# Layer 1 attention of a four-layer gated model: scores made once with queries in partitions, weights turned by TensorE

## The chip, the cores and the metric

The kernel runs on one core of a Trainium2 chip. The metric is the device time of one execution in microseconds. The engines are TensorE (PE, with its weight loads as PEld), VectorE (DVE), ScalarE (ACT), GpSimd (POOL) and SyncE (SP), which issues most DMAs. Profiles come from one profiled execution.

## What is computed

Eight batches of 256 query rows by 128 features (`x`) run through four layers. Each adds a gated cross attention over 512 context rows of its batch, and then a gated feed-forward part:

```python
x = x + tanh(g_xattn[0]) * L0_xattn(layernorm(x), ctx, ctx, ...)
x = x + tanh(g_ffn[0])   * L0_ffn(layernorm(x), ...)      # experts, top 2 of 8
x = x + tanh(g_xattn[1]) * L1_xattn(layernorm(x), ctx, ctx, ...)
x = x + tanh(g_ffn[1])   * L1_ffn(layernorm(x), rhs)      # int8 product
...                                                       # layers 2 and 3
```

The change is in `L1_xattn`: 16 heads of 64 features. With query, key and value projections with biases, it is softmax(QK^T / 8) V over the 512 keys for each head and query, and then the output projection with its bias. Everything is f32.

## The kernel before

**Stages.** Layer 0's attention and its experts come first, to about 320 us. During them and into the next stage, the keys and values of layer 1 are projected for all batches and stored in DRAM (`fill`, `k1`, `v1`). After that `pipeline` runs layers 1, 2 and 3 as one loop of steps.

**Units, steps and half steps.** A unit is a layer, a batch `b` and a half `g` of the heads. In layer 1 a unit has eight heads, as four pairs `j`. A unit takes four steps, and a step has two half steps. So a batch of layer 1 is two units, eight steps, 16 half steps, and a pair of heads takes one step. Three streams run side by side: `prepare` (query projections, key and value loads) first, `largest` (the scores' maxima) four steps later, and `attend` (weights and values) eight steps later. One step issues:

```python
next(streams["at"]); self.run_due()      # half step 1: attend; work that is due
next(streams["la"]); self.run_soon()     # maxima; sums and reciprocals
self.some(self.front); self.some(self.back)
next(streams["at"]); next(streams["pr"]) # half step 2: attend; one projection
next(streams["la"]); self.fill2(1)
self.some(self.front); self.some(self.back)
```

`front` is the work ahead of the next batch (`ahead`: gather layer 0's expert rows, add them to `x`, layer normalisation, turn the rows by TensorE in `rows_turned`). `back` is the feed-forward part of a batch that is done (`int8`: normalise, largest per row, round, turn by TensorE, product, add). Both are generators that are advanced one piece in each half step. All instructions of TensorE, VectorE, ScalarE and GpSimd in the pipeline are kept in program order on their engine, and each engine works in order.

**Layer 1 before.** `largest` makes the scores with queries in partitions (`sc<-kx,qx`: 64-row matmuls for the two heads of a pair, 512 keys), and VectorE takes the negated maximum over the keys (`nm<-sc`). Every two pairs, `largest_rows` turns these maxima by TensorE (`pj<-c_f,nm`), splits them into a rounded high part and a rest (`ms`) and writes them by four small DMAs as rows of a tile `m4`. `attend` makes the scores a second time with keys in partitions: a matmul with the constant `up` puts the (negated) maxima of each query into the PSUM tile (`sc<-m,up`), and the scores are added to it (`sc<-qx,kx`). One exponential on ScalarE with a scale of 1/8 gives the weights `et` (`et<-sc`, 128x1024), keys in partitions, as the value matmuls need them. GpSimd adds the weights up (`k<-et`, `total<-k`). A step later `values_of_pair` multiplies by the values (`av<-et,va`), multiplies the totals by ones to sum over partitions (`av<-total,ones`), and VectorE takes the reciprocal and scales (`rec<-av`, `aT`). When both halves of a batch are done, `output1` projects (`pj<-wb,aT`), adds to `x` and hands the batch to `int8`.

**Buffers.** PSUM holds three `sc` tiles of 128x1024, one `pj` and one `av`. `pj` serves query projections (`pj<-xT,wb`, evacuated by ScalarE as `qx<-pj`), transposes of rows, of `nm` and of the int8 rows, the int8 product, and the output projection. A tile is used again when its last reader is done.

Of the kernel before, what the change touches and what calls it, by code (L numbers as in the profile page):

```python
# [31 lines left out]
def bcast(ap, shape):  # L32
    return ap.to_broadcast(list(shape))
# [15 lines left out]
class Flamingo:  # L49
# [60 lines left out]
    def load(self):  # L110
        nc, a = self.nc, self.a
        self.x = self.const("x", [P, NT, D])
        self.ctxT = self.const("ctxT", [D, NB * SK])
        xs = a["x"].rearrange("(t p) d -> p t d", p=P)

        def rows(b):
            nc.sync.dma_start(self.x[:, 2 * b : 2 * b + 2, :], xs[:, 2 * b : 2 * b + 2, :])

        def context(b, eng=nc.sync):
            eng.dma_start(self.ctxT[:, b * SK : (b + 1) * SK], a["ctxT"][:, b * SK : (b + 1) * SK])  # L120


        rows(0)
        context(0, nc.scalar)
        self.w0 = self.loaded("w0", eng=nc.scalar, pool=self.wf0)
        self.b0 = self.loaded("b0", [1, 512], src=a["b0"].unsqueeze(0), eng=nc.scalar, pool=self.wf0)
        self.c_f32 = self.loaded("c_f32")
        self.ident = self.c_f32[:, 0:128]
        self.tri = self.c_f32[:, 128:256]
        self.iota = self.c_f32[:, 256:385]  # L130
        self.up2 = self.c_f32[:, 385:513]
        self.row = self.c_f32[:, 513:514]
        self.g = self.loaded("g", [P, 8], src=a["g"].partition_broadcast(P))
        rows(1)

        self.w1 = self.weights_tile().rearrange("p (k n) -> p k n", k=4)
        self.w1_b = self.loaded("w1_b", eng=nc.scalar)
        nc.sync.dma_start(self.w1[:, 1, :], a["w1"][:, 1, :])
        nc.sync.dma_start(self.w1[:, 2, :], a["w1"][:, 2, :])
        for b in range(2, 4):  # L140
            rows(b)
        for b in range(1, 4):
            context(b)
        for b in range(4, NB):
# [771 lines left out]
    def pipeline(self):  # L916
        nc, tc = self.nc, self.tc
        with ExitStack() as st:
# [3 lines left out]
            self.p_av = st.enter_context(tc.tile_pool(name="p_av", bufs=1, space=PS))  # L922
            self.po = st.enter_context(tc.tile_pool(name="pipe", bufs=2))
            units = [(layer, b, g) for layer in (1, 2, 3) for b in range(NB) for g in range(2)]
            self.due, self.soon, self.back, self.front, self.step, self.kept = [], [], [], [], 0, {}
            streams = {
                n: self.chain(f, units, wait)
# [45 lines left out]
    def run_soon(self):  # L973

        now, self.soon = self.soon, []
        for f in now:
            f()

    def later(self, steps, f):
        self.due.append((self.step + steps, f))  # L980

# [4 lines left out]

    def setup(self, pool):
        nc, a, one = self.nc, self.a, self.one
        self.up = self.t(one, "up", [P, P], F32R)
        nc.vector.tensor_copy(self.up, self.up2)  # L990
        tri8 = self.t(pool, "tri8", [P, 2, SK], U8)
        nc.sync.dma_start(tri8, a["keep_qk"].rearrange("(c p) k -> p c k", p=P))
        self.triq = self.t(one, "triq", [P, 2, SK], BF16)
# [23 lines left out]
        pt = self.pj16()  # L1017
# [106 lines left out]
    def prepare1(self, n, b, g):  # L1124
        nc = self.nc
        xT = self.kept["xT", 1, b]
        qT = self.t(self.po, "qx", [P, 4, S], bufs=3)
        kT = self.t(self.po, "kx", [P, 4, SK], bufs=3)
        self.kept[n] = [qT, kT, None]
        for j in range(4):  # L1130
            f = 4 * g + j
            if j == 0:
                nc.sync.dma_start(kT, self.k1[n])
            if j == 1:
                va = self.kept[n][2] = self.t(self.po, "va", [P, 4, 512], bufs=3)
                nc.sync.dma_start(va, self.v1[n])
            pq = self.pj()
            self.mm2(pq[:, 0:S], self.w1[:, 0, f * P : (f + 1) * P], xT)
            nc.scalar.activation(
                qT[:, j, :], pq[:, 0:S], AF.Identity, bias=self.w1_b[:, 0, f : f + 1]  # L1140
            )
            yield

    def largest(self, n, layer, b, g):
        if layer > 1:
            yield from self.largest23(n, layer, b, g)
            return
        nc = self.nc
        qT, kT, _ = self.kept[n]

        mr = self.t(self.po, "m4", [P, 4, S], bufs=3)
        nc.gpsimd.memset(mr, 0.0)
        self.kept[n][3:] = [mr]
        nm = self.t(self.po, "nm", [P, 2, 2, 2, 2])
        for j in range(4):
            for c in range(2):
                ps = self.sc()
                for z in range(2):
                    h = slice(64 * z, 64 * z + 64)
                    self.mm(ps[:, z, :], qT[h, j, c * P : (c + 1) * P], kT[h, j, :])  # L1160
                nc.vector.tensor_reduce(nm[:, c, j // 2, :, j % 2], ps, AX.X, ALU.max, negate=True)
                if c and j % 2:
                    self.later(1, self.largest_rows(
                        nm, j // 2, 1.0, lambda z, k: mr[64 * z + k : 64 * z + k + 1]
                    ))
                yield

    def largest_rows(self, m, half, scale, row):
# [20 lines left out]
    def attend(self, n, layer, b, g):  # L1189
        if layer > 1:  # L1190
            yield from self.attend23(n, layer, b, g)
            return
        nc = self.nc
        qT, kT, va, mr = self.kept[n]
        mr = mr.bitcast(F32R)
        aT = self.t(self.po, "aT", [P, 4, S], bufs=3)
        self.kept["aT", g] = aT
        for j in range(4):
            ets = []
            half = self.t(self.po, "k4", [P, 2, 2, S])  # L1200
            for k2 in range(2):
                ps = self.sc()
                for z in range(2):
                    h = slice(64 * z, 64 * z + 64)
                    self.mm(
                        ps[:, z, :], self.up[h, :],
                        bcast(mr[h, j, :].unsqueeze(1), [64, 2, S]), True, False,
                    )
                for c in range(2):
                    for z in range(2):  # L1210
                        h = slice(64 * z, 64 * z + 64)
                        self.mm(
                            ps[:, z, c * S : (c + 1) * S],
                            kT[h, j, (2 * k2 + c) * P : (2 * k2 + c + 1) * P], qT[h, j, :],
                            False, c == 1,
                        )
                ets.append(self.weights(ps, 0.125))
                nc.gpsimd.tensor_tensor(half[:, k2], ets[k2][:, :, 0, :], ets[k2][:, :, 1, :], ALU.add)
                if k2:
                    self.later(1, self.values_of_pair(b, 4 * g + j, ets, half, va, aT))  # L1220
                yield

    def weights(self, ps, scale):
        et = self.t(self.po, "et", [P, 2, 2, S], bufs=6)
# [2 lines left out]
        )  # L1227
        return et

    def values_of_pair(self, b, f, ets, half, va, aT):  # L1230
        nc = self.nc
        both = [self.kept["aT", 0], aT]
        total = self.t(self.po, "total", [P, 2, S])
        nc.gpsimd.tensor_tensor(total, half[:, 0], half[:, 1], ALU.add)

        def run():
            po = self.av()
            for c in range(4):
                for z in range(2):
                    at = 64 * (2 * (f % 4) + z)  # L1240
                    self.mm(
                        po[64 * z : 64 * z + 64, 0:S], va[:, c, at : at + 64],
                        ets[c // 2][:, z, c % 2, :], c == 0, c == 3,
                    )
            self.soon.append(lambda: scaled(po))

        def scaled(po):
# [215 lines left out]
    def attend23(self, n, layer, b, g):  # L1463
# [9 lines left out]
        held = {}  # L1473
        for j in range(4):
            for k2 in range(2):
                ps = self.sc()
                for z in range(2):
                    self.mm(
# [249 lines left out]
def arrays_of(i):  # L1728
# [9 lines left out]
            np.eye(P, dtype=f),  # L1738
            (p[:, None] <= p[None, :]).astype(f),
            np.tile(np.arange(P + 1, dtype=f), (P, 1)),  # L1740
            np.tile((p[:, None] % 64 < 2).astype(f), (1, P)),
            p[:, None].astype(f),
        ],
        axis=1,
# [90 lines left out]
```

## Time and profile before

| | us |
|---|---|
| median of 3 runs (range) | 1806.87 (1792.55 to 1807.64) |
| profiled execution | 1792.19 |
| its span, first to last instruction | 1790.4 |
| PE busy in the span | 1558.7 (87%) |
| DVE busy | 1163.2 (65%) |
| ACT busy | 750.8 (42%) |
| POOL busy | 742.8 (41%) |
| mean granted TensorE clock | 0.934 |

In the profile's rows `out<-in` names the tile that is written and those that are read; `L863` and `L867` are the helpers that issue every matmul and every transpose, and `L46` is the one through which the instructions of the other engines go. So groups are told apart by their tiles. An f32 matmul shows as two matmuls. Matmuls overlap, so the pace of TensorE is read from start to start and not from the durations. The first attention of layer 1 begins at about 373 us, and layer 1's last output projection is at 960.7 us.

### The profile page before, as it was taken

How to read it: one execution, taken by the hardware profiler on the slowest of the kernel's cores; microseconds unless marked ns; L12 is line 12 of the kernel's file. 1: busy time of each engine (PE TensorE's matmuls, PEld its weight loads, DVE VectorE, ACT ScalarE, POOL GpSimd, SP SyncE). 2: the span in 40 equal slices, each digit the busy share in tenths (PEclk: the TensorE clock that was granted, in tenths of full speed). 3: DMA queues.
4: the chain of work that ended last, by engine and by line, in shares of the span. 5: the costliest groups of instructions: out<-in, count | busy, mean ns of one | idle time of the engine just before them, and what ended most of it. 6: DMA issues, size and time to landing. Idle time of an engine off the chain costs nothing.

```text
span 1790.4 us, 32118 instructions
## 1 busy us (share of the span) xinstructions
PE 1558.7 (87%) x11760; PEld 773.9 (43%) x11856; DVE 1163.2 (65%) x2667; ACT 750.8 (42%) x1244; POOL 742.8 (41%) x1140
## 2 busy tenths in 40 slices
PE   6886578789999999999998888889889999899995
PEld 2332226234545445445454444445444444444442
DVE  6997542145677676586776686475565665677774
ACT  3553233333233233232333455555545555455543
POOL 4896221234566566465554123232332322422211
PEclk9887688899999999999999899999989999899997
DMA  5443232723121122121222332222121211222210
GB/s 191 157 170 114 86 127 77 227 106 107 53 97 54 49 78 78 48 54 49 72 51 94 72 78 65 49 71 62 39 54 32 58 32 36 53 58 62 67 27 25
DMA packets 65409, 137.77 MB, mean 77 GB/s; under 512 B 12370, under 2 KB 28003, under 8 KB 58596
## 3 DMA queue, kind: packets, MB, share of 16 engines
q1 hardware_dynamic: 63282, 132.03, 23.8%
q0 software_dynamic: 1536, 3.15, 1.3%
q8 instruction: 94, 1.54, 0.4%
q10 hardware_dynamic: 434, 0.54, 0.1%
q14 instruction: 63, 0.52, 0.1%
HBM read 83.50 MB, written 51.38 MB: 75 GB/s over the span
## 4 chain that ended last, share of the span: by engine, by line
PE 58%; DVE 20%; POOL 7%; issue 7%; ACT 5%; DMA 2%; SPq 0%; ACTq 0%; DVEq 0%; POOLq 0%
PE sc L863 31%; PE av L863 13%; PE pj L863 8%; DVE junk L46 5%; PE pj L867 3%; DVE rec L46 2%; PE fl L863 2%; DVE ps L46 2%; DVE pj L46 2%; DVE x L46 2%; DVE nm L46 1%; ACT et L46 1%; POOL lnz L46 1%; DMA kx<-k 1%; POOL k L46 1%
## 5 line engine op out<-in xcount | busy, mean ns | idle before, releaser
L46 ACT ACTIVATE et<-sc 128x1024 f32<-128x1024 f32 (+1 forms) x403 | 405.1, 1005 | 465.0 <-PE sc L863 418.0
L46 DVE CUSTOM_DVE_ANT_0 junk<-sc,m 128x512 bf16<-128x512 f32 x512 | 351.0, 686 | 43.8 <-PE sc L863 30.2
L863 PE MATMUL sc<-qx,kx 64*128 64x256 f32 (+2 forms) x2048 | 269.1, 361 | 13.4 <-DMA qx<-ms 3.1
L863 PE MATMUL sc<-kx,qx 64*128 64x512 f32 (+2 forms) x1024 | 268.9, 561 | 0.7 <-ACT et L46 0.7
L863 PE MATMUL av<-et,va 128*32 128x256 f32 (+1 forms) x3072 | 265.7, 408 | 0.8 <-DVE aT L46 0.8
L863 PEld LDWEIGHTS sc<-qx,kx 64*128 64x128 f32 (+2 forms) x2048 | 179.6, 191 | 139.3 <-issue 120.8
L46 POOL TENSOR_TENSOR k<-et 128x512 f32<-128x512 f32 x128 | 162.6, 1272 | 176.8 <-ACT et L46 174.1
L46 DVE TENSOR_REDUCE nm<-sc 128x2 f32<-128x1024 f32 x128 | 156.1, 1219 | 110.2 <-PE sc L863 110.2
L863 PEld LDWEIGHTS av<-et,va 128*32 128x32 f32 (+1 forms) x3072 | 133.8, 125 | 101.1 <-issue 35.4
L46 POOL TENSOR_TENSOR x<-row,x 128x256 f32<-128x256 f32 x76 | 55.5, 730 | 274.1 <-ACT row L46 260.7
L863 PE MATMUL sc<-m,identb 128*128 128x512 bf16 x416 | 139.7, 400 | 22.0 <-DVE mx L46 12.2
L46 DVE SCALAR_TENSOR_TENSOR ms<-pj,ms 4x256 fp32r<-4x256 f32 x96 | 39.6, 412 | 169.4 <-ACT ms L46 163.1
L863 PEld LDWEIGHTS sc<-kx,qx 64*128 64x128 f32 (+2 forms) x1024 | 87.4, 185 | 87.6 <-issue 66.0
L46 POOL TENSOR_TENSOR lnz<-lny 128x2 f32<-128x2 f32 (+1 forms) x129 | 25.2, 195 | 211.8 <-DVE lny L46 198.4
L46 DVE RECIPROCAL rec<-av 128x256 f32<-128x256 f32 x64 | 111.9, 1748 | 0.0
L46 DVE SCALAR_TENSOR_TENSOR x<-sc,comb,x 128x128 f32<-128x128 f32 x128 | 39.0, 346 | 100.4 <-ACT row L46 100.4
L46 ACT ACTIVATE total<-sc,f_b 128x512 f32<-128x512 f32 x64 | 44.0, 688 | 107.7 <-PE sc L863 107.7
L863 PE MATMUL sc<-xT,wb 128*64 128x512 f32 x256 | 68.9, 614 | 19.0 <-DVE x L46 17.1
L46 POOL TENSOR_TENSOR total<-k 128x512 f32<-128x512 f32 x64 | 81.5, 1273 | 5.0
L863 PEld LDWEIGHTS sc<-wb,total 128*64 128x64 f32 x1024 | 61.6, 137 | 33.6 <-issue 32.6
L863 PE MATMUL sc<-m,up 64*128 64x512 f32 x256 | 75.4, 584 | 0.0
L46 POOL TENSOR_TENSOR aT<-aT,rec 128x512 f32<-128x512 f32 x16 | 20.4, 1273 | 131.8 <-DVE rec L46 131.8
(275 smaller groups left out, 2280.1 us busy)
## 6 DMA issues: line engine op xcount, KB each, us to landing
kx<-k SPq DMA_DIRECT2D x16, 1024.0 KB
va<-v SPq DMA_DIRECT2D x16, 1024.0 KB
k<-fill SPq DMA_DIRECT2D x46, 256.0 KB
v<-fill SPq DMA_DIRECT2D x45, 256.0 KB
pd<-k SPq DMA_DIRECT2D x16, 512.0 KB
kx<-pd SPq DMA_DIRECT2D x64, 128.0 KB
kx<-pd SPq DMA_DIRECT2D x128, 64.0 KB
qx<-pd SPq DMA_DIRECT2D x128, 64.0 KB
```

The source lines that it names most:

```text
L46: return lambda *args, **kw: self.tc.keep_in_program_order(v(*args, **kw))
L863: self.nc.tensor.matmul(out, lhsT, rhs, start=start, stop=stop)
L867: self.tc.keep_in_program_order(self.nc.tensor.transpose(out, in_, ident))
```

## The change

Layer 1's `largest` stream issues nothing; it only keeps its place in the order. `attend` makes the scores once per half step, with queries in partitions: one half `c` of the 256 queries, two heads, 512 keys. VectorE takes the negated maximum, and ScalarE makes the weights with it as a bias, one exponential for each head, into a tile of the `m4` buffers. The division by 8 moves into the query projection (`scale=0.125`, with a scaled bias `bq1`). Two half steps later `turned` transposes these weights by TensorE, eight blocks of 128x128, into an `sc` tile. ScalarE copies that to `et`, and GpSimd adds up in two instructions. In layer 2's `attend23` a call `turn(1)` works off what is left. The values are made for 128 queries at a time. The constant `up2`, the tile `up`, the memset of the rows and layer 1's call of `largest_rows` are gone.

```diff
+    def turn(self, n):
+        if len(self.turns) >= n:
+            self.turns.pop(0)()
...
+        if n == 0:
+            self.bq1 = self.t(self.one, "bq1", [P, 8])
+            nc.gpsimd.tensor_scalar(self.bq1, self.w1_b[:, 0, :], 0.125, None, ALU.mult)
...
             nc.scalar.activation(
-                qT[:, j, :], pq[:, 0:S], AF.Identity, bias=self.w1_b[:, 0, f : f + 1]
+                qT[:, j, :], pq[:, 0:S], AF.Identity, bias=self.bq1[:, f : f + 1], scale=0.125
             )
...
     def largest(self, n, layer, b, g):
...
+            for _ in range(8):
                 yield
...
     def attend(self, n, layer, b, g):
...
+            held = {}
+            for c in range(2):
+                self.turn(2)
                 ps = self.sc()
                 for z in range(2):
                     h = slice(64 * z, 64 * z + 64)
-                    self.mm(
-                        ps[:, z, :], self.up[h, :],
-                        bcast(mr[h, j, :].unsqueeze(1), [64, 2, S]), True, False,
-                    )
-                for c in range(2):
-                    for z in range(2):
-                        h = slice(64 * z, 64 * z + 64)
-                        self.mm(
-                            ps[:, z, c * S : (c + 1) * S],
-                            kT[h, j, (2 * k2 + c) * P : (2 * k2 + c + 1) * P], qT[h, j, :],
-                            False, c == 1,
-                        )
-                ets.append(self.weights(ps, 0.125))
-                nc.gpsimd.tensor_tensor(half[:, k2], ets[k2][:, :, 0, :], ets[k2][:, :, 1, :], ALU.add)
-                if k2:
-                    self.later(1, self.values_of_pair(b, 4 * g + j, ets, half, va, aT))
+                    self.mm(ps[:, z, :], qT[h, j, c * P : (c + 1) * P], kT[h, j, :])
+                nm = self.t(self.po, "nm", [P, 2])
+                nc.vector.tensor_reduce(nm, ps, AX.X, ALU.max, negate=True)
+                p = self.t(self.po, "m4", [P, 4, S], bufs=3).rearrange("p (z k) s -> p z (k s)", z=2)
+                for z in range(2):
+                    nc.scalar.activation(p[:, z, :], ps[:, z, :], AF.Exp, bias=nm[:, z : z + 1])
+                self.turns.append(self.turned(c, p, held, (b, 4 * g + j, va, both)))
                 yield
+
+    def turned(self, c, p, held, of_pair):
+        nc = self.nc
+        def run():
+            ps = self.sc()
+            pt = ps.rearrange("p a (k z s) -> p (a k) z s", k=2, z=2)
+            for k in range(4):
+                for z in range(2):
+                    self.tp(pt[:, k, z, :], p[:, z, k * P : (k + 1) * P], self.ident)
+            et = self.t(self.po, "et", [P, 2, 2, S], bufs=6)
+            nc.scalar.copy(et.rearrange("p a k s -> p (a k s)"), ps.rearrange("p a n -> p (a n)"))
+            held[c] = et.rearrange("p a k (z s) -> p (a k) z s", z=2)
+            if c == 0:
+                held["half"] = self.t(self.po, "k4", [P, 2, 2, S])
+                held["total"] = self.t(self.po, "total", [P, 2, S])
+            half = held["half"][:, c]
+            nc.gpsimd.tensor_tensor(half, et[:, 0], et[:, 1], ALU.add)
+            half = half.rearrange("p k (z s) -> p k z s", z=2)
+            nc.gpsimd.tensor_tensor(
+                held["total"][:, :, c * P : (c + 1) * P], half[:, 0], half[:, 1], ALU.add
+            )
+            if c:
+                self.later(1, self.values_of_pair(held, *of_pair))
+        return run
...
     def values_of_pair(...):
...
-            for c in range(4):
-                for z in range(2):
-                    at = 64 * (2 * (f % 4) + z)
-                    self.mm(
-                        po[64 * z : 64 * z + 64, 0:S], va[:, c, at : at + 64],
-                        ets[c // 2][:, z, c % 2, :], c == 0, c == 3,
-                    )
+            for c in range(2):
+                for k in range(4):
+                    for z in range(2):
+                        at = 64 * (2 * (f % 4) + z)
+                        self.mm(
+                            po[64 * z : 64 * z + 64, c * P : (c + 1) * P], va[:, k, at : at + 64],
+                            held[c][:, k, z, :], k == 0, k == 3,
+                        )
...
     def attend23(...):                      # layers 2 and 3
+                self.turn(1)
                 ps = self.sc()
```

More of the change, by code (lines that the diff above doesn't have):

```diff
@@ L130, in load @@
         self.iota = self.c_f32[:, 256:385]
-        self.up2 = self.c_f32[:, 385:513]
-        self.row = self.c_f32[:, 513:514]
+        self.row = self.c_f32[:, 385:386]
         self.g = self.loaded("g", [P, 8], src=a["g"].partition_broadcast(P))
@@ L924, in pipeline @@
             units = [(layer, b, g) for layer in (1, 2, 3) for b in range(NB) for g in range(2)]
+            self.turns = []
             self.due, self.soon, self.back, self.front, self.step, self.kept = [], [], [], [], 0, {}
@@ L988, in setup @@
         nc, a, one = self.nc, self.a, self.one
-        self.up = self.t(one, "up", [P, P], F32R)
-        nc.vector.tensor_copy(self.up, self.up2)
         tri8 = self.t(pool, "tri8", [P, 2, SK], U8)
@@ L1146, in largest @@
             yield from self.largest23(n, layer, b, g)
[L1147 to L1155, printed above, removed]
-            for c in range(2):
-                ps = self.sc()
-                for z in range(2):
-                    h = slice(64 * z, 64 * z + 64)
[L1160 to L1165, printed above, removed]
+        else:
+            for _ in range(8):
                 yield
@@ L1193, in attend @@
         nc = self.nc
-        qT, kT, va, mr = self.kept[n]
-        mr = mr.bitcast(F32R)
+        qT, kT, va = self.kept[n]
         aT = self.t(self.po, "aT", [P, 4, S], bufs=3)
         self.kept["aT", g] = aT
+        both = [self.kept["aT", 0], aT]
         for j in range(4):
-            ets = []
-            half = self.t(self.po, "k4", [P, 2, 2, S])
-            for k2 in range(2):
+            held = {}
+            for c in range(2):
+                self.turn(2)
                 ps = self.sc()
@@ L1204, in attend @@
                     h = slice(64 * z, 64 * z + 64)
-                    self.mm(
-                        ps[:, z, :], self.up[h, :],
-                        bcast(mr[h, j, :].unsqueeze(1), [64, 2, S]), True, False,
-                    )
-                for c in range(2):
-                    for z in range(2):
-                        h = slice(64 * z, 64 * z + 64)
-                        self.mm(
-                            ps[:, z, c * S : (c + 1) * S],
-                            kT[h, j, (2 * k2 + c) * P : (2 * k2 + c + 1) * P], qT[h, j, :],
-                            False, c == 1,
-                        )
@@ L1228, in weights, with values_of_pair @@
         return et
-    def values_of_pair(self, b, f, ets, half, va, aT):
+    def values_of_pair(self, held, b, f, va, both):
         nc = self.nc
-        both = [self.kept["aT", 0], aT]
-        total = self.t(self.po, "total", [P, 2, S])
-        nc.gpsimd.tensor_tensor(total, half[:, 0], half[:, 1], ALU.add)
+        total, aT = held["total"], both[-1]
         def run():
             po = self.av()
-            for c in range(4):
-                for z in range(2):
-                    at = 64 * (2 * (f % 4) + z)
-                    self.mm(
-                        po[64 * z : 64 * z + 64, 0:S], va[:, c, at : at + 64],
-                        ets[c // 2][:, z, c % 2, :], c == 0, c == 3,
-                    )
+            for c in range(2):
[6 more added lines that the diff above has]
+                        )
             self.soon.append(lambda: scaled(po))
@@ L1740, in arrays_of @@
             np.tile(np.arange(P + 1, dtype=f), (P, 1)),
-            np.tile((p[:, None] % 64 < 2).astype(f), (1, P)),
             p[:, None].astype(f),
```

## The prediction

> **What bounds the kernel now.** The page's first rows come first: TensorE is busy 87% of the span, VectorE 65%, ScalarE 42%, GpSimd 41%. An average over stages says little, so next the stretches. Layer 1's outputs (`pj<-wb,aT`, 64 matmuls) stand at 537.4, 608.7 and 680.0 us in the chain that ended last, one batch (8 steps, 16 half steps) per 71.3 us. The busy times of two such stretches, columns PE, PEld, DVE, ACT, POOL, granted clock, DMA share, GB/s:
>
> ```profile
> 546.25:617.59 71.34, 67.02 (x496) 35.22 (x496) 50.91 (x67) 21.54 (x31) 43.23 (x58) 1.00 0.21 64
> 688.92:760.26 71.34, 67.02 (x475) 35.24 (x476) 48.48 (x65) 21.07 (x30) 43.22 (x58) 0.95 0.21 64
> ```
>
> TensorE is busy 67.0 of 71.3 us, so it sets the pace; ScalarE, 21.5, is nearly free. Its waits there are 2.0 us on `xn`, 1.5 us on `row`, 0.8 us on `ql`. One plain step follows in the timeline; starts are what counts, since durations overlap:
>
> ```profile
> 554.04 1.13 PE L863 MATMUL sc<-kx,qx 64*128 64x512 f32 x4
> 554.61 0.80 PE L863 MATMUL sc<-m,up 64*128 64x512 f32 x2
> 555.24 1.02 PE L863 MATMUL sc<-qx,kx 64*128 64x256 f32 x8
> 556.20 1.95 PE L863 MATMUL av<-et,va 128*64 128x256 f32 x16
> 558.07 1.13 PE L863 MATMUL sc<-kx,qx 64*128 64x512 f32 x4
> 559.13 0.65 PE L863 MATMUL av<-total,ones 128*64 128x256 f32 x4
> 559.72 0.50 PE L863 MATMUL sc<-m,up 64*128 64x512 f32 x2
> 560.05 1.02 PE L863 MATMUL sc<-qx,kx 64*128 64x256 f32 x8
> 561.01 0.65 PE L863 MATMUL pj<-xT,wb 128*64 128x256 f32 x4
> ```
>
> From one query projection (553.46) to the next (561.01) is 7.55 us. Start to start: scores for the largest 1.06, rows of the largest plus second scores 1.29, values 1.87, sums 0.59, projection 0.58.
>
> **The change, part by part.**
>
> *TensorE.* Per half step the `up` matmuls and the second scores go (1.29 us, or 1.1 behind a first score). Eight f32 transposes of 128x128 come. Nearest rows:
>
> ```profile
> 884.69 0.44 PE L867 MATMUL pj<-c_f,xn 128*128 128x128 f32 x2
> 892.91 0.62 PE L867 MATMUL pj<-identb,m 128*128 128x128 bf16 x8
> ```
>
> A lone f32 transpose takes 0.33 us, a pair 0.44, so one more costs 0.11; eight bf16 ones take 0.62, so a run of eight is pipelined. Eight f32: 0.87 plus about 0.16 for the change of shape (between groups above), 1.03 us. The Trainium skill, "TensorE: Matmul & The Clock Gate", Part 4, gives about 275 ns for a transpose in a kernel's context and says that transposes do not count as activity for the full clock. By that rule eight cost 2.2 us, 1.2 us more in each of 128 half steps, +150 us if nothing hides it; by the row, nothing. I take the row: it has eight in one run. The rule stays as the upper end.
> Values become 32 matmuls of 128 columns instead of 16 of 256. The output projection has that shape: 64 in 3.64 us, so 32 take 1.82. No change. A step is then 2x1.03 + 2x1.06 + 1.87 + 0.59 + 0.58 = 7.22 us: **2.6 us less per batch**. Four pairs of transposes of the largest go too, 0.31 us each: **1.25 us less**.
>
> *ScalarE.* One exponential of 1024 (1.02) becomes two of 512 with a bias, by `total<-sc,f_b` 0.69 each, and a copy of 1024, by `m<-pj` 1.01: 2.4 us per half step, 4.8 per step, plus 0.47 for the query copy. It fits in 7.2 as a sum; its order does not (below). *VectorE* keeps its 128 maxima (1.22 us) and loses the 0.41 us halves. *GpSimd*: two of (1.27 + 0.73) per step against three of 1.27; 0.2 us more, beside other work. 128 small DMAs of rows, the memsets (0.95 us) and 64 KB of constants go; they were off the path, I count 0.
>
> *The new wait.* Before, the maxima fed rows that were needed four steps later. Now one half step runs in one chain: scores, maximum (VectorE), two exponentials, all before the next instruction on ScalarE. There, in program order, the query copy `qx<-pj` stands **behind both exponentials**; before, it stood behind one that waited for TensorE alone. It frees `pj`, of which there is one buffer. Whoever uses `pj` right after the projection holds up TensorE, in order, with all behind it. In each batch three do, all in second half steps: the int8 transposes (`pj<-identb,ql`), the int8 product (`pj<-qr,qlT`), and the transposes of the next batch's rows (`pj<-c_f,xn`).
>
> Count from the end of the sums (`av<-total,ones`). TensorE reaches the `pj` user after 1.03 + 1.06 + 0.58 = 2.67 us. ScalarE frees `pj` after reciprocal 1.75, `aT` 0.42, VectorE's side work F that stands before the maximum, maximum 1.22, exponentials 1.38, query copy 0.47, four hand-overs of 0.07: 5.5 + F. The stop is 2.85 + F:
> - int8 product: F = first guess of the root, 0.65. Stop **3.5 us**.
> - rows: F = two `xn`, 1.4 to 2.5. Stop **4.8 us**.
> - int8 transposes: F = two adds of gathered rows (`x<-xT,w,x`, 1.2 each) and two roundings, 2.9. Stop 5.7, and 2 more because the half step before has the other two adds ahead of its own maximum: **7.7 us**.
>
> Together 16.0 us per batch. The present waits of 4.3 us are at the same places or go with the transposes of the largest. Batch: 71.3 - 2.6 - 1.25 - 4.3 + 16.0 = **79.2 us, +7.9**. Elsewhere slack covers the chain: `sc` rotates over three, and a score waits for the copy of the transposes one half step back; from the end of a score to that copy's end is 0.07+1.22+0.07+1.38+0.07+1.01 = 3.8 us, against 6.2 us of TensorE work between (1.87 + 0.59 + 2x1.03 + 1.06 + 0.58).
>
> *The clock.* In layer 3 there is a stop like these:
>
> ```profile
> 1556.26 0.48 PE L867 MATMUL pj<-c_f,xn 128*128 128x128 f32 x1 [3.66 <-POOL xn L46]
> 1558.30 0.80 PE L863 MATMUL sc<-qx,kx 34*128 34x256 f32 x4
> 1567.19 0.50 PE L863 MATMUL sc<-qx,kx 34*128 34x256 f32 x4
> ```
>
> After 3.66 us idle the four score matmuls take 0.80 instead of 0.50, until about 1565. The same page ("Why this matters for your kernels") asks for no gaps over about 3 us; here already 1.54 us before 987.64 (on `ql`) was followed by some 6.5 us of doubled durations. By the page one or two of the three stops lower the clock, by the trace all. A slow period of 6.8 us loses 3.4 us of TensorE work; part falls into waits that exist anyway. I take 2.3 per stop, 7 per batch (0 to 12). Batch: **86.2, +14.9**.
>
> *Ends.* Steps 4 to 7 held eight scores for the largest before any attention; a step took 5.55 us there (350.26 to 355.80), against 3.1 in the steps before. Four such: -10. Filling the first batch without stops: -3. Where layer 2's maxima begin while layer 1 attends, VectorE gets eight maxima of 1.22 on top, with transposes left over for layer 2's first step: +8. Six full batches: 6 x 14.9 = 89.
> Sum: 89 - 10 - 3 + 8 = **+84 us**. The profiled execution took 1792.2 us (span 1790.4): **1876 us**. The median of the runs shown, 1806.9, lies 0.8% above it, the lowest run (1792.6) at it; so this is 3.8% over the median, and runs may scatter some 15 us up.
>
> **The rivals.**
> 1. *Stops, but the clock holds.* For it: 546 to 689 us stays at 1.00 despite waits of 1.5 us. Against: the stop of 3.66. 6 x 7.9 - 5 = +42: 1834 us. 0.20.
> 2. *Transposes are slow or do not count as activity.* Against: eight in 0.62. For: no row shows 16 f32 ones in each step; with the stops, TensorE's counted work would be near half the time and the low clock the rule. +25 per batch, -5: 1937 us. 0.15.
> 3. *The sum of TensorE decides, faster.* `pj` is freed in time because VectorE runs ahead. Then 8 x 3.85 + 10 goes: 1751 us. Against: reciprocal and `aT` alone put the maximum 2.2 us after the sums. This turns slower once the stops exceed 3.85 + 4.3 us a batch. 0.07.
> 4. *Stops half as long* (1.5 to 4 us), the clock mostly held: +0 to +20, 1800 us. 0.10.
> 5. That it does not do what it says: the changed kernel's own instruction order shows the copies, exponentials and `qx` as counted here. Not counted.
>
> **How the numbers follow.** The forecast has 0.48. Its own range: stops 12 to 20 us, clock 3 to 12 per batch, 1840 to 1915. The 8-in-10 range takes in rival 1 and most of 2 and 4: 1812 to 1938. About 1% (18 us) can be told from no change. Faster by over 1%: 0.07; within: 0.09 (most of rival 4); slower: 0.84.
>
> **What would show it.** Layer 1's outputs some 80 to 90 us apart instead of 71.3. Waits of TensorE at `pj<-identb,ql`, `pj<-qr,qlT`, `pj<-c_f,xn` on ScalarE's `qx`, 12 us or more per batch. Transposes of `p` in groups of eight of about 1.1 us. Granted clock in layer 1 clearly under 1.00, ScalarE busy near 45 us a batch. The forecast is wrong if those waits stay under 5 us a batch, or if a group of eight takes over 1.6 us at full clock. Layers 2 and 3 should keep their time.

## The result, and the profile after

The changed kernel takes **1865.7 us** (median of 4 runs, 1861.7 to 1866.0) against 1804.4 us of the kernel before (1792.6 to 1807.6), measured beside it: a ratio of **1.035**, interval 1.030 to 1.040. Predicted were 1876 us and "slower" with 0.84. The profiled executions are 1861.7 us after and 1792.2 us before. The experiments below ran in three sets, each beside the kernel before, whose medians there were 1800.3 to 1802.5 us.

The first three rows of the page after, busy time and share of the span:

```profile
span 1859.8 us, 33621 instructions
## 1 busy us (share of the span) xinstructions
PE 1565.8 (84%) x12560; PEld 838.3 (45%) x12560; DVE 1140.0 (61%) x2634; ACT 888.6 (48%) x1468; POOL 738.6 (40%) x1189
```

TensorE's share fell, although the span grew: it waits more. Two batches of layer 1, from one output (`pj<-wb,aT`) to the next; columns are start and end, length, busy PE, PEld, DVE, ACT, POOL, granted clock, DMA share, GB/s:

```profile
562.45:644.37 81.92, 68.69 (x584) 44.56 (x584) 48.08 (x63) 39.15 (x59) 42.84 (x64) 0.87 0.16 56
644.37:726.29 81.92, 68.70 (x584) 44.56 (x584) 48.07 (x63) 39.14 (x59) 42.82 (x64) 0.87 0.17 56
```

A batch takes 81.9 us instead of 71.3. Idle time rose from 4.3 to 13.2 us, and the granted clock fell to 0.87, so that the busy 68.7 us hold less work than they seem to. What TensorE waited for, 480 to 900 us (total, times, longest):

```profile
PE pj L866 <- ACT qx L46: 43.8, 10, 4.5
PE pj L862 <- ACT qx L46: 16.0, 11, 2.7
PE sc L866 <- ACT m L46: 2.9, 5, 0.6
PE av L862 <- POOL total L46: 2.8, 5, 0.6
```

60 of 66 us stand at `pj`, released by ScalarE's query copy `qx`. The same batch in TensorE's timeline (start, duration, what, and in brackets the idle time before it):

```profile
568.27 1.09 PE L866 MATMUL sc<-c_f,m 128*128 128x128 f32 x8
569.29 1.13 PE L862 MATMUL sc<-kx,qx 64*128 64x512 f32 x4
570.35 0.65 PE L862 MATMUL pj<-xT,wb 128*64 128x256 f32 x4
570.93 1.09 PE L866 MATMUL sc<-c_f,m 128*128 128x128 f32 x8
571.96 1.13 PE L862 MATMUL sc<-kx,qx 64*128 64x512 f32 x4
573.01 1.97 PE L862 MATMUL av<-et,va 128*64 128x128 f32 x32
574.81 0.60 PE L862 MATMUL av<-total,ones 128*64 128x256 f32 x4
575.35 1.09 PE L866 MATMUL sc<-c_f,m 128*128 128x128 f32 x8
...
598.16 0.37 PE L866 MATMUL pj<-identb,ql 128*128 128x128 bf16 x2 [4.23 <-ACT qx L46]
598.32 1.91 PE L866 MATMUL sc<-c_f,m 128*128 128x128 f32 x8
600.16 2.08 PE L862 MATMUL sc<-kx,qx 64*128 64x512 f32 x4
...
610.29 0.37 PE L862 MATMUL pj<-qr,qlT 128*128 128x128 bf16 x2 [2.73 <-ACT qx L46]
...
624.98 0.69 PE L866 MATMUL pj<-c_f,xn 128*128 128x128 f32 x2 [4.54 <-ACT qx L46]
```

The first seven rows are one plain step, from 568.27 to the start of the eighth at 575.35: 7.08 us; it was 7.55. A group of eight transposes occupies 1.02 us, start to start. Then come the three stops of the prediction, 11.5 us together, each followed by rows of twice the duration (1.91 for 1.09, 2.08 for 1.13).

### The profile page after: what moved, and what is told of

It reads as the page before. It is cut to its first block, busy times and chain, and to the rows that moved or that the text cites. A ratio compares the mean times of both kernels' runs of the same rounds, so it can differ in the third digit from the quotient of the medians.

```text
span 1859.8 us, 33621 instructions
## 1 busy us (share of the span) xinstructions
PE 1565.8 (84%) x12560; PEld 838.3 (45%) x12560; DVE 1140.0 (61%) x2634; ACT 888.6 (48%) x1468; POOL 738.6 (40%) x1189
## 3 DMA queue, kind: packets, MB, share of 16 engines
q8 instruction: 100, 1.64, 0.4%
## 4 chain that ended last, share of the span: by engine, by line
PE 44%; DVE 17%; ACT 6%; POOL 4%; issue 4%; DMA 1%; SPq 1%; ACTq 0%; DVEq 0%; POOLq 0%
PE sc L862 20%; PE av L862 12%; PE pj L862 5%; DVE junk L46 4%; DVE rec L46 3%; PE sc L866 3%; DVE nm L46 3%; PE pj L866 2%; ACT m L46 2%; POOL lnz L46 1%; DVE x L46 1%; DVE xn L46 1%; ACT total L46 1%; ACT et L46 1%; POOL k L46 1%
## 5 line engine op out<-in xcount | busy, mean ns | idle before, releaser
L46 ACT ACTIVATE et<-sc 128x1024 f32<-128x1024 f32 (+1 forms) x275 | 273.8, 996 | 147.1 <-PE sc L862 140.8
L862 PE MATMUL av<-et,va 128*64 128x128 f32 (+1 forms) x4096 | 278.6, 356 | 0.0
L46 ACT ACTIVATE m<-sc,nm 128x512 f32<-128x512 f32 x256 | 162.2, 687 | 205.2 <-DVE nm L46 196.1
L862 PEld LDWEIGHTS av<-et,va 128*64 128x64 f32 (+1 forms) x4096 | 188.6, 134 | 109.3 <-issue 67.5
L46 ACT COPY et<-sc 128x1024 f32<-128x1024 f32 x128 | 130.2, 1017 | 103.2 <-PE sc L866 96.1
L866 PE MATMUL sc<-c_f,m 128*128 128x128 f32 x1024 | 155.7, 301 | 3.6 <-ACT m L46 2.9
L866 PEld LDWEIGHTS sc<-c_f,m 128*128 128x128 f32 x1024 | 125.1, 154 | 50.1 <-issue 38.4
L862 PE MATMUL sc<-qx,kx 38*128 38x256 f32 (+1 forms) x1024 | 133.5, 339 | 0.4 <-DMA qx<-ms 0.4
L862 PEld LDWEIGHTS sc<-qx,kx 38*128 38x128 f32 (+1 forms) x1024 | 79.4, 191 | 114.3 <-issue 110.7
L46 POOL TENSOR_TENSOR total<-k 128x256 f32<-128x256 f32 x128 | 93.1, 727 | 10.0
```

The lines of the kernel that those rows point to most:

```text
L46: return lambda *args, **kw: self.tc.keep_in_program_order(v(*args, **kw))
L862: self.nc.tensor.matmul(out, lhsT, rhs, start=start, stop=stop)
L866: self.tc.keep_in_program_order(self.nc.tensor.transpose(out, in_, ident))
```

## The experiments

Theory: the stops come from the query copy queued behind the second half step's exponentials, which wait for VectorE; the stops then bring the half-rate periods. Rivals: TensorE's clock costs nothing beside the waits; the transposes lower the clock; ScalarE's added work binds by itself.

### 1. The projection ahead of the second half step

```diff
-                next(streams["at"])
-                next(streams["pr"])
+                if self.step < 4 * 2 * NB:
+                    next(streams["pr"])
+                    next(streams["at"])
+                else:
+                    next(streams["at"])
+                    next(streams["pr"])
```

> The changed kernel with one edit: while layer 1 lasts, a step's query projection is issued ahead of its second half step of attention instead of behind it. On ScalarE the query copy `qx<-pj` then stands behind the exponentials of the first half step only, and `pj` is free well before the second half step's users come. My theory (the stops come from the query copy queued behind the second half step's exponentials, and the stops bring the half-rate periods): the three stops of 4.2, 2.7 and 4.5 us per batch go under 1 us each, the three half-rate periods per batch go, a batch falls from 81.9 to 63 to 66 us (81.9 - 11.5 - 7.5 = 62.9), the run to about 1735 to 1765 us, under the kernel before. Rival A (transposes and ScalarE's extra work bind, whatever the order): the wait only moves, to `sc` or to the transposed weights, a batch stays over 78 us and the run at 1840 us or more. Rival B (the first half step's exponentials, themselves behind VectorE's side work, hold the query copy as well): stops half as long, 70 to 75 us per batch, about 1800 us.

Measured: **1761.4 us** (1759.9 to 1763.3), ratio to before 0.978 (0.972 to 0.983). Two batches of it, columns as above, then its waits from 480 to 860 us:

```profile
538.40:601.85 63.45, 59.93 (x584) 40.32 (x582) 46.50 (x62) 39.06 (x60) 42.75 (x65) 1.00 0.22 72
601.85:666.93 65.08, 61.57 (x585) 41.20 (x583) 46.50 (x62) 39.06 (x60) 42.72 (x65) 0.97 0.21 70
```

```profile
PE pj L866 <- POOL ql L46: 8.9, 5, 1.8
PE av L862 <- POOL total L46: 4.6, 5, 0.9
PE pj L866 <- DVE xn L46: 4.0, 10, 0.4
```

No wait on `qx` is left, the clock is back, and a batch takes 63.4 us, 18.5 less: 9.7 from waits (13.2 to 3.5), 7.6 from the clock (run 4), and 8 steps of 0.15 us (6.93 from 544.12 to 551.05 against 7.08). ScalarE has the same work, 39.1 us a batch, and there are as many transposes. Rival A falls, and rival B too.

### 2. The exponentials without VectorE's maximum

```diff
-                nc.vector.tensor_reduce(nm, ps, AX.X, ALU.max, negate=True)
...
-                    nc.scalar.activation(p[:, z, :], ps[:, z, :], AF.Exp, bias=nm[:, z : z + 1])
+                    nc.scalar.activation(p[:, z, :], ps[:, z, :], AF.Exp)
+                nc.vector.tensor_reduce(nm, p, AX.X, ALU.max, negate=True)
```

> The changed kernel without the link from VectorE to ScalarE: the exponentials take no bias, and VectorE's maximum (same count and size) is taken from the exponentials' output instead, where nobody waits for it. What is left out: the subtraction of the largest. The order on every engine and all loads stay. My theory (a stop is maximum plus VectorE's side work plus two exponentials plus the query copy): each stop shrinks to about 1.4 us, what two exponentials (1.38) and the copy (0.47) leave beyond the projection; 3 x 1.4 = 4.2 us of stops per batch, the clock loss 0 to 7.5 us: a batch 67 to 75 us, the run 1770 to 1820 us. Rival (ScalarE's own added work of 2.4 us per half step makes the stops, VectorE has no part): stops stay over 3 us each, over 79 us per batch, 1850 us.

Measured: 1761.3 us (1759.0 to 1763.8). One batch:

```profile
596.54:664.51 67.97, 62.82 (x585) 40.34 (x583) 48.03 (x62) 37.21 (x59) 42.77 (x64) 0.97 0.21 67
```

68.0 us, inside 67 to 75: the order on ScalarE alone leaves stops of 1.0 us at most on `qx`, and the link to VectorE makes the rest of them. The run as a whole came out 9 us under the range that I expected, because the first batch (83.7 us for 104.3, from layer 1's ninth projection, where attention begins, to its first output) and the passage to layer 2 (73.3 for 78.9) got shorter as well. The rival (ScalarE's work alone) falls.

### 3. Extra matmuls in the stops, too many

```diff
+    def busy(self, n):
+        ps = self.sc()
+        for k in range(n):
+            self.mm(ps[:, k % 2, :], self.ident[0:64, :], self.ctxT[0:64, 0:512])
...
+        self.busy(7)
         pt = self.pj16()
...
+        self.busy(4)
         po = self.pj()
...
+        if b:
+            self.busy(8)
         self.rows_turned(layer, b, xn)
```

> The changed kernel with 7, 4 and 8 extra f32 matmuls of 64x512 (about 0.53 us each, their result unused) issued just ahead of the int8 transposes, the int8 product and the next rows' transposes, so that TensorE works through most of each stop instead of idling. The waits for `pj` stay as they are. My theory (idle time at the stops brings the half-rate periods, which cost 7.5 us per batch beside the 11.5 us of waiting): granted clock in layer 1 back to 0.95 or more, a batch about 75 us, the run 40 to 50 us shorter, 1815 to 1825 us. Rival 1 (the waiting alone is the loss, the clock costs nothing because VectorE and ScalarE are late anyway): 81.9 us per batch as now, 1862 us or a little more. Rival 2 (transposes don't count as activity and the low clock comes from them): half-rate periods stay, 1860 us or more.

Measured: 1872.4 us (1868.7 to 1879.3), which looks like rival 1. The timeline says otherwise: seven of the extra matmuls took 6.2 us, 0.89 each, not 0.53. My 0.53 came from pairs of scores that use rows 0 to 63 and 64 to 127 in turn; these used the same 64 rows each time. So 16.9 us of extra work stood where the stops were 11.5, 5.4 too much; yet a batch took 79.5 us, 2.4 less. In the profiled total this was lost again: 10 us up to the first output of layer 1 (490.8 us for 480.8), and 16 us behind its last output, where eleven of the extra matmuls stand at places that had no such stop. Inconclusive as a total, so it was sized anew.

### 4. Extra matmuls that fit

```diff
-        self.busy(7)
+        self.busy(4)
...
-        self.busy(4)
+        self.busy(2)
...
-            self.busy(8)
+            self.busy(5)
```

> The run with extra matmuls ahead of the three users of `pj`, sized anew: there one took 0.89 us instead of the 0.53 I had counted, so they filled 16.9 us where the stops were 11.5. Now 4, 2 and 5 of them, 9.8 us, a little under the stops of 4.2, 2.7 and 4.5 us. My theory (the stops bring the half-rate periods): what remains idle at each stop is under 1 us, granted clock 1.00, a batch 74 to 75 us (81.9 less the 7.5 lost to the clock), the run 1810 to 1830 us. Rival 1 (the clock costs nothing beside the waits): 81 to 82 us per batch, 1860 to 1870 us.

Measured: 1828.4 us (1819.9 to 1838.4), 37 us under the changed kernel. One batch:

```profile
633.03:707.32 74.29, 71.10 (x604) 43.53 (x604) 48.07 (x63) 39.12 (x59) 42.84 (x64) 1.00 0.18 61
```

The 9.8 us of extra matmuls and what is left of waits at `pj` (8.2 us in five batches, 1.6 each) fill the same 11.4 us as the stops did. VectorE's, ScalarE's and GpSimd's times are those of the changed kernel to 0.1 us. Only the clock differs, 1.00 for 0.87, and the batch is **7.6 us shorter**. That is the price of the half-rate periods. Rival 1 falls.

### 5. Transposes by themselves

```diff
             self.ternary_end()
+            for groups, columns in ((40, 128), (20, 512), (80, 128), (20, 512)):
+                for n in range(groups):
+                    ps = self.sc()
+                    for k in range(8 if columns == 128 else 2):
+                        if columns == 128:
+                            self.tp(ps[:, k // 4, (k % 4) * P : (k % 4 + 1) * P], self.ctxT[:, k * P : (k + 1) * P], self.ident)
+                        else:
+                            self.mm(ps[:, k, :], self.ident[0:64, :], self.ctxT[0:64, 0:512])
```

The rule and the price named here are those that the prediction takes from the Trainium skill, "TensorE: Matmul & The Clock Gate", Part 4: transposes that don't count as activity, and about 275 ns for one.

> The kernel before, with a tail behind its last instruction: 40 groups of eight f32 transposes of 128x128, 20 pairs of f32 matmuls of 64x512, 80 groups of eight transposes, 20 pairs of matmuls; results unused. It measures what a group of eight costs when nothing else is mixed in, and whether transposes alone raise and hold the clock. By the row of the trace (eight in about 1.05 us at full clock, and they count as activity): the 80 groups in 80 to 90 us at a granted clock of 1.00, the first 40 in under 50 us. By the rule that they don't count: the clock falls to half some us into the 80 groups, a group takes about 2 us and the 80 take 150 us or more, and the first 40 stay at half, about 80 us. By the price of 275 ns each at full clock: 176 us for the 80. The run is longer than before by the tail, 170 to 350 us.

The tail in TensorE's timeline, and three stretches of it (clock in the third column from the end):

```profile
1800.57 36.83 PE L867 MATMUL sc<-c_f,ctxT 128*128 128x128 f32 x320
1871.86 70.08 PE L867 MATMUL sc<-c_f,ctxT 128*128 128x128 f32 x640
```

```profile
1800.57:1810.00 9.43, 9.43 (x73) 9.43 (x72) 0.63 (x2) 0.00 (x0) 0.00 (x0) 0.81 0.11 32
1810.00:1837.33 27.33, 27.33 (x251) 27.16 (x250) 0.00 (x0) 0.00 (x0) 0.00 (x0) 1.00 0.01 1
1900.00:1941.87 41.87, 41.87 (x385) 41.70 (x383) 0.00 (x0) 0.00 (x0) 0.00 (x0) 1.00 0.01 1
```

One run, 1979.2 us. 80 groups took 70.0 us, 0.88 each, with 1.00 granted throughout; I had expected 80 to 90 us from rows that include a change of shape, and 0.87 is what the prediction gave without it. The first 40 came after a stretch at half clock (0.50 from 1790 to 1800.57 us) and reached 1.00 within 10 us, with nothing but transposes running. Transposes of f32 raised and held the clock here, so the measurement decides against the page's statement that they don't count, and against rival 2 of the prediction. The 275 ns are another matter. The page gives them for a bf16 transpose in one kernel's context, and the profile gives one f32 transpose nearly the same duration, 272 ns as the median of these 960. But such rows overlap: from start to start one takes 109 ns in this run and 128 ns in the changed kernel's groups of eight. The prediction's upper end, eight for 2.2 us, multiplied a duration where the pace counts.

### 6. The same order in the kernel before

The edit of experiment 1 on the kernel before.

> The kernel before with the same edit as the run with the early projection. There the query copy stands behind an exponential that waits for TensorE alone, so the place of the projection should not matter: my theory expects 1790 to 1815 us, 70 to 72 us per batch, no difference that can be told. Rival: the early projection is what makes that run fast, whatever the softmax: 64 to 66 us per batch and 1760 us here too.

Measured: 1775.0 us (1771.6 to 1776.1), ratio 0.985 (0.982 to 0.988). **My theory missed this**: I expected no difference. A batch takes 66.9 us for 71.3. Of the 4.4 us, some 1.6 are waits (21.6 us in five batches before, 13.8 here), and 8 x 0.36 are the plain step, 7.19 from projection to projection for 7.55. The projection now stands behind the sums, and one half step's scores directly ahead of the next one's. The 0.36 us are found at just these places, start to start: sums 0.48 for 0.59, projection 0.53 for 0.58, second scores 0.86 for 0.96, scores for the largest 0.46 for 0.57. That the neighbour is the reason is argued, not tested apart. So against the 104 us that the order brings the changed kernel stand some 27 (1.5%) that it brings without the change. The rival falls as well, since the batch stays 3.4 us over that of the changed kernel.

### 7. The passage to layer 2

```diff
         mx = self.t(self.po, "mx", [P, 2, 2, 2, 2])
+        if n == 2 * NB:
+            nc.gpsimd.memset(mx, 30000.0)
...
-                for z in range(2):
+                for z in range(2 if n > 2 * NB else 0):
```

> The changed kernel with the early projection, and without VectorE's part of layer 2's first unit of maxima (16 operations of 0.7 us; a constant stands in their place, so that unit's largest is left out). It tests the passage from layer 1 to layer 2, where the last two outputs of layer 1 stand 77.4 us apart instead of 63.4. My theory (VectorE holds there both the maximum that the exponentials wait for and layer 2's, 1.5 us more per half step in the same queue, and the score tiles come free late): 64 to 69 us there, the run 8 to 13 us shorter, about 1750 us. Rival (the passage is long for other reasons, layer 2's own TensorE work and the slow clock at its start): 75 us or more and no shorter run.

Measured: 1746.3 us (1741.5 to 1750.0), 15 us under the run it is built on. The passage there:

```profile
858.35:920.63 62.28, 61.21 (x598) 40.06 (x596) 45.02 (x69) 36.23 (x55) 40.94 (x69) 1.00 0.22 49
```

62.3 us for 77.4. In the changed kernel itself, with its own order, the passage and its waits, 958 to 1037 us, are

```profile
958.00:1037.00 79.00, 69.22 (x596) 44.51 (x596) 54.45 (x101) 36.59 (x55) 40.79 (x68) 0.89 0.18 40
```

```profile
PE sc L862 <- DVE mx L46: 4.0, 2, 3.3
PE sc L862 <- ACT m L46: 3.8, 4, 2.4
```

Layer 2's maxima delay the maximum that layer 1's exponentials wait for, a score tile comes free late, and the clock falls again. The rival falls.

### 8. GpSimd beside VectorE's adds

```diff
             self.ternary_end()
+            ...
+            add = lambda out: nc.vector.scalar_tensor_tensor(
+                out[:, 0:128], a[:, 0:128], self.place_w[:, 0, 0:1], a[:, 128:256], ALU.mult, ALU.add
+            )
+            for _ in range(24):
+                add(c)
+            nc.gpsimd.tensor_tensor(g[:, 0:128], c[:, 0:128], a[:, 512:640], ALU.add)
+            for _ in range(12):
+                nc.gpsimd.tensor_tensor(g[:, 512:1024], a[:, 0:512], a[:, 512:1024], ALU.add)
+            for _ in range(24):
+                add(d)
```

> The kernel before with a tail behind its last instruction: 24 adds on VectorE (128x128, two operands in SBUF, the form of the gathered adds) while GpSimd is idle, then 24 more while GpSimd runs 12 additions of 128x512 back to back; results unused. In the kernel before such an add took 1.26 us and in the changed one 0.35. If GpSimd's run holds VectorE's two-operand adds up, the first 24 take 0.3 to 0.5 us each and the second ones are held to about one per GpSimd operation (1.0 us or more each) until GpSimd is done; if not, both take the same.

The first 24 adds alone; adds beside GpSimd; adds behind it:

```profile
1800.64:1810.04 9.40, 0.00 (x0) 0.00 (x0) 8.58 (x26) 0.00 (x0) 0.00 (x1) 0.50 0.10 28
1810.45:1826.50 16.05, 0.00 (x0) 0.00 (x0) 15.62 (x13) 0.00 (x0) 15.19 (x13) 0.50 0.00 0
1826.50:1830.52 4.02, 0.00 (x0) 0.00 (x0) 3.66 (x11) 0.00 (x0) 0.00 (x0) 0.50 0.00 0
```

One run, 1833.3 us. Counts at the edges of a stretch include neighbours. 24 adds in 9.40 us are 0.39 each; beside GpSimd only about 13 pass in 16.05 us, one per GpSimd operation, 1.2 us each; afterwards 11 in 4.02. The Trainium skill, "GPSIMD Engine Reference", Specifications, says that GpSimd shares its SBUF interface with VectorE and contends with instructions that have two SBUF inputs; this run agrees, with 1.2 us for 0.39.

### 9. The early projection in all layers

```diff
-                next(streams["at"])
-                next(streams["pr"])
+                next(streams["pr"])
+                next(streams["at"])
```

> The changed kernel with the projection ahead of the second half step in all three layers, not in layer 1 alone. In the kernel before, the same order gave 4.5 us per batch in layer 1, 1.5 of it from waits and the rest from 0.36 us less per step, because two scores now follow each other without a change of shape. If layers 2 and 3 have the same kind of loss: 1740 to 1755 us. Rival: there the exponentials wait for TensorE alone and the place of the projection costs nothing: within 5 us of 1761.

Measured: 1786.8 us (1780.2 to 1795.2), 25 us over the run that has it in layer 1 alone. Both expectations missed. From 940 to 1740 us TensorE waits 11.0 us at `pj` on `ACT m` (2.4 in that run) and 5.3 us on `DVE ms` (none there). Those are 14 of the 33 us between the two profiled executions. The granted clock there is 0.93 for 0.95 as well; over 800 us that is some 16 us of full clock, an estimate from these two rounded figures, and about what remains. In layers 2 and 3 the projection itself arrives at `pj` too soon.

### 10. What the change is worth with that order

> The changed kernel with the early projection in layer 1 once more, beside the kernel before with that same order on the same chip: what the change itself is worth when the query copy doesn't stand behind the exponentials. By the outputs of layer 1, 63.45 us against 66.88 per batch, less 14 us lost in the passage to layer 2: 6 to 20 us faster than that kernel, 1755 to 1765 us. Rival: the change is worth nothing but its order, both at 1765 to 1775 us.

> The kernel before with the early projection, for that comparison: 1770 to 1780 us.

Measured: 1762.0 us (1753.3 to 1767.5) with the change, ratio to before 0.979 (0.975 to 0.982); 1773.8 us (1765.2 to 1787.1) without it, ratio 0.984 (0.980 to 0.988). The 12 us are in the expected 6 to 20. Single runs overlap, and so do the two intervals; but the means of these five and six runs, on one chip, are 1760.9 and 1775.1 us, 14 us apart with a 95% interval of 4 to 24, and the earlier pair (experiments 1 and 6) stood at 1761.4 and 1775.0. So the changed kernel with the early projection **is faster than the kernel before in either order**, by about 1% where the order is the same. Most of the gain is the order's: 26 of 38 us come without the change.

## Why the prediction was right, point by point

The predicted sum, beside what the two profiled executions differ by (from when the projections and outputs of layer 1 start):

| stretch | predicted, us | measured, us |
|---|---|---|
| ahead of the first projection | 0 | +13.8 |
| steps ahead of attention | -10 | -15.2 |
| first batch, filling | -3 | +16.2 |
| six batches | +89 | +46.0 |
| passage to layer 2 | +8 | +15.7 |
| layers 2 and 3 | 0 | -7.1 |
| sum | +84 | +69.4 |

The total is closer than its terms, and part of that is luck: the six batches were put 43 us too high, and the entry, the first batch and the passage together 41 us too low. The -7.1 of layers 2 and 3 is scatter: in seven profiled executions that leave their work unchanged they took 823 to 831 us from layer 1's last output on. Of the signs named, ScalarE's time per batch is off as well, 39.1 us for some 45; the waits, the groups of eight and the distance of the outputs came near the forecast.

- **Ahead of the first projection.** Not the change: the profiled execution of before entered there at 334.2 us, but four other executions of programs that equal it up to that point at 343 to 352 us, the changed kernel at 348.0. The prediction started from an early entry. Without this term the profiles differ by 56 us; the medians differ by 61.
- **Place, cause and form of the stops: right.** `pj`, freed by `qx`, at the three users named (experiments 1 and 2).
- **Their size: too large**, 16.0 for 11.5. Product and rows, 3.5 and 4.8, came out at 2.73 and 4.54. The mis-sized term is the stop at the int8 transposes, 7.7 for 4.23. VectorE and ScalarE ahead of it, after:

```profile
591.75 1.75 DVE L46 RECIPROCAL rec<-av 128x256 f32<-128x256 f32 x1
593.53 0.42 DVE L46 TENSOR_TENSOR aT<-av,rec 128x256 f32<-128x256 f32 x1
593.88 0.97 DVE L46 SCALAR_TENSOR_TENSOR x<-xT,w,x 128x128 f32<-128x128 f32 x2
594.77 0.28 DVE L46 TENSOR_SCALAR r<-xn,li 128x128 f32<-128x128 f32 x1
595.08 0.23 DVE L46 TENSOR_SCALAR r<-r 128x128 f32<-128x128 f32 x1
595.23 1.22 DVE L46 TENSOR_REDUCE nm<-sc 128x2 f32<-128x1024 f32 x1
```

```profile
596.48 1.26 ACT L46 ACTIVATE m<-sc,nm 128x512 f32<-128x512 f32 x2 [2.25 <-DVE nm L46]
597.63 0.47 ACT L46 ACTIVATE qx<-pj,bq 128x256 f32<-128x256 f32 x1
```

  The chain is as predicted: reciprocal, `aT`, side work, maximum, exponentials, query copy. But the side work F, 593.88 to 595.23, is 1.35 us and not 2.9: 2.85 + 1.35 is 4.2. I took 1.2 us per gathered add from before, where the median of 20 was 1.26; after it is 0.35. In before such adds stand beside GpSimd's additions:

```profile
571.96 2.31 DVE L46 SCALAR_TENSOR_TENSOR x<-xT,w,x 128x128 f32<-128x128 f32 x2
571.51 1.26 POOL L46 TENSOR_TENSOR k<-et 128x512 f32<-128x512 f32 x1
572.85 1.27 POOL L46 TENSOR_TENSOR total<-k 128x512 f32<-128x512 f32 x1
```

  Experiment 8 shows that this alone makes an add that long. The 2 us that I added for the half step before were not in the stop; 0.59 and 0.17 us appeared ahead of two scores instead.
- **The clock: right.** 7 us per batch predicted, 7.6 measured (experiment 4), three half-rate periods per batch. After a stop of 2.73 us durations doubled, as the trace of before suggested and the 3 us of the Trainium skill ("TensorE: Matmul & The Clock Gate", "Why this matters for your kernels") did not. Two readings behind it were off: all three predicted stops are over those 3 us, not "one or two", and the slow period behind 987.64 us lasts 10.2 us in the granted clock, not some 6.5.
- **TensorE's sum: nearly right.** The plain step was put at 7.22 and is 7.08; the step fell by 0.47 us, 3.8 per batch, not 2.6. With the measured terms (and 1.25 as predicted) a batch is 71.3 - 3.8 - 1.25 - 4.3 + 13.2 + 7.6 = 82.8, against 81.9.
- **Six batches: the multiplication was wrong too.** Before's last three intervals were 74.4, 73.0 and 70.1 us, not 71.3, and the sixth after has no next rows: 68.2 us, with 5.6 us of waits. So 6 x 14.9 should have been about 5 x 10 and nothing.
- **First batch: the term that failed.** "Filling the first batch without stops" forgot a queue: while it fills, the keys and values of layer 1 are copied out of `sc` by ScalarE, behind the exponentials and the query copy as well. One such place, the copy and TensorE's wait for it:

```profile
401.13 0.60 ACT L46 ACTIVATE et<-sc 128x512 f32<-128x512 f32 x1
401.79 1.08 PE L862 MATMUL sc<-ctxT,wb 128*64 128x512 f32 x4 [2.10 <-ACT et L46]
```

  In before this wait is 0.75. From 376 us to the first output TensorE waits 14.7 us on `ACT et` (4.5 before), and a stop of 4.5 at `pj` comes to it.
- **Passage: right in kind, half in size**, 8 for 15.7: a wait in the score tiles and a slow clock came to it (experiment 7).

## What to carry to other kernels

When an instruction gets a new input from another engine, list what stands behind it in its own queue, and which single buffers those free; here a copy of 0.47 us that had become late cost 11.5 us of waits and 7.6 us of clock per batch. Before rejecting a change that adds such a wait, move the short instruction ahead of it: the same change was 3.5% slower in one order and 2.2% faster in another, and the same move on the old kernel tells how much of that is the change. A duration taken from a trace belongs to what ran beside it.

## What the runs showed of the hardware that was not expected

- VectorE's 128x128 adds with both operands in SBUF go one per GpSimd operation while GpSimd runs additions of 128x512 back to back: 1.2 us instead of 0.39.
- f32 transposes alone brought the granted clock from half to full within 10 us and held 1.00 for 70 us.
- A 64-row f32 matmul of 512 columns took 0.89 us where the same 64 rows were used each time (experiment 3), and 0.53 us in pairs of scores that use the two halves of the rows in turn. The operands differ too, so the halves as the reason are argued.
- A stop of 2.73 us was enough for a half-rate period; stops of 1.8 us a batch in experiment 1 left one batch at 1.00 and the next at 0.97. The granted clock in the traces shows much of what decides. From about 480 us on, all 60 half-rate periods in the profiles of before, after and experiment 1 begin, within each profile, on a grid of 3.41 us and last one, two or three of its intervals. While layer 1 runs, an interval in which TensorE was busy for less than 1.6 us was followed by half rate, and one with more than 1.7 us by full rate (at 1.61 to 1.64 us both occurred); full rate came back only behind an interval without a pause. So the same stop counts or not by where it falls on the grid. A batch of 81.92 us is 24 intervals, so every batch met the grid alike. In layers 2 and 3 half rate followed intervals with up to 3.0 us of busy time too, so busy time as the profile counts it is not the whole rule.
